# Cross-attention on one core: the order of a slot's work, of its fill and of its end

## The chip, the cores and the metric

The kernel runs on one core of a Trainium2 chip. The metric is the time of one execution on the device in microseconds (us). Several executions are timed and their median is given; one more execution is profiled, and its page and trace are what is read here. The engines are called TensorE (PE, with its weight loads PEld), VectorE (DVE), ScalarE (ACT), GpSimd (POOL) and SyncE (SP), which issues most of the DMAs.

## The reference, cut to what matters

```python
# x: (32, 512, 640) float32, read as hidden_states: 32 batches, 512 rows, 640 columns
# ctx_2048: (32, 77, 1024); all 77 tokens are text, so the other three attentions have no keys
q = _heads(hidden_states @ to_q_w)                      # 20 heads of 32
h_txt = _sdpa(q, _heads(ehs_txt @ to_k_w), _heads(ehs_txt @ to_v_w))   # softmax over 77 keys
out = _merge(h_txt) @ to_out_w + to_out_b
out = out + residual                                    # residual = hidden_states
```

In and out are float32. The kernel gets near that precision by splitting each operand into a high and a low part and adding three products (high x high, high x low, low x high).

## The kernel before

**Tiles and slots.** After a first part that computes the keys and values of all 32 batches and writes them to scratch memory (`k_dram`, `v_dram`; groups of 512 context rows, `LAST` the fifth and shorter one), the kernel walks through 160 slots: `b, j = divmod(n, 5)`, where b is the batch and j one of five chunks of 128 columns, that is four heads. One call of `slot(n)` issues, for chunk n, the scores and exps of four query tiles of 128 rows, and around them work of other chunks, so that the engines overlap:

- `queries(n + 1, ...)`: 15 products into the bank `pq`; `split_q(n + 1)` then makes `qt`: a copy on ScalarE, two partition-crossing copies on GpSimd (L458) and two subtractions on VectorE (L460). `scores(n + 1, 0)` at the head of the next slot needs all of them.
- `scores(n, t)`, t = 0 to 3: three products into a tile `sc` (three buffers), and the row maximum `nm` on VectorE; `exps(n, t)`: four activations on ScalarE that also sum the rows (`sms`).
- `sums(n - 1)`: the reciprocal `rs` on VectorE. `normalize(n - 1, rs)`: one multiplication of `pn` by it on GpSimd (L511). `transpose_p(n - 1)`: VectorE transposes `pn` into `z`, and SyncE stores it in four DMAs to `pd`.
- `load_p(n - 3)`: SyncE loads that chunk back, transposed, into `raw` (two buffers). In the next slot this chunk is `taken` (`takes`: four slots after its scores): `cast_p` (ScalarE, a small and a large cast into `pp`, one buffer), `last_p` (GpSimd, L556: the low part of the small piece), `rest_p` (VectorE, L549: the low part of the large piece), then `values(taken)`.
- `values(m)`: six products into the bank `pa` (one buffer), in the order of `PASSES`: passes 1 and 2 need the casts, 3 and 4 need `last_p`, 5 and 6 need `rest_p`. `sum_a(m)`: a copy `aw` on ScalarE (L581) and two additions on VectorE (L583). In the next slot `high_a(m)` (ScalarE, L590) and `low_a(m)` (VectorE, L595) split the result into `at` and free the bank.
- The output projection: `piece(b, i)` issues products of `at` and `wo_s` into `po` (L613), two pieces per slot; `PIECES` tells which of an earlier batch. The first piece of j=3 ends with the chunk taken in the slot before. `finish()` adds `po` to the residual rows `xr` on VectorE (L642) and stores them.
- `load_residual(b, t)`: SyncE loads 128 rows of x into `xr` (L602, three buffers), one of the four t in each of the slots j=1, 3, 4 and 0 (`RESIDUAL`). `add_bias(b, t)`: GpSimd adds the output bias to them (L606), in the slots that `BIAS` names.
- For the next batch: `refill` issues the key and value loads of half the heads or segments at two places of a slot (`load_keys` eight, `load_values` eight DMAs a group), `copy_keys` copies keys on GpSimd (L423, L424), `load_x`, `transpose_x` and `split_x` prepare its queries' operand.

**What sets the order.** The order is written out by hand: under `tc.manual_schedule` every engine executes its instructions as the program issues them, and SyncE issues its DMAs in that order, each after the one eight before it has landed. The tables show the assignment to slots (a pair is how many batches back, and which t):

```python
RESIDUAL = {1: (1, 0), 3: (1, 1), 4: (1, 2), 0: (2, 3)}
BIAS = {2: (1, 0), 4: (1, 1), 0: (2, 2), 1: (2, 3)}
```

**Fill and end.** The first three slots also compute values of the last context group (`beside`, `context_values`). `LATE` = 3 is the first slot that uses the tiles of the later stage. From slot 8 on there is output work as well (`has_out`). `end()` works off what is left after slot 159: the last four chunks' casts, values and projections.

Of the kernel before, what the change touches and what calls it, by code (L numbers as in the profile page):

```python
# [8 lines left out]
F32 = mybir.dt.float32  # L9
FPR = mybir.dt.float32r  # L10
AF = mybir.ActivationFunctionType
ALU = mybir.AluOpType
# [11 lines left out]
P = 128  # L24
# [27 lines left out]
def kernel(  # L52
# [154 lines left out]
    def split_keys(g, j):  # L207
        g0, gn = GROUPS_KV[g]
        ks = kvt.tile([P, 2, G], FPR, tag="ks", name="ks")
        split(ks[:, 0, :gn], ks[:, 1, :gn], pks.pop(j)[:, :gn])  # L210
        engine = nc.gpsimd if g + 1 < len(GROUPS_KV) else nc.sync
        j0 = GROUPS[GROUP_OF[j]][0]
        engine.dma_start(
            k_dram[GROUP_OF[j]][:, :, j - j0, g0 : g0 + gn].bitcast(F32), ks[:, :, :gn].bitcast(F32)
        )
# [177 lines left out]
    raws, pps, ats, pds, sms, pqs, pas, xrs, pos = ({} for _ in range(9))  # L393
# [115 lines left out]
    def normalize(n, rs):  # L509
        pf = pnb[n % 2][:, :, :NKEY]  # L510
        nc.gpsimd.tensor_tensor(  # L511
            pf, pf, rs.unsqueeze(2).to_broadcast([P, NQ * HPC, NKEY]), ALU.mult
        )
# [24 lines left out]
    def cast_p(n):  # L538

        raw = raws[n]  # L540
        pp = late[0].tile([P, 5, S], FPR, tag="pp", name="pp", bufs=1)
        nc.scalar.copy(pp[:64, 4, :], raw[:64, 2, :])  # L542
        nc.scalar.copy(pp[:, 0:2, :], raw[:, 0:2, :])  # L543
        pps[n] = pp
# [19 lines left out]
    def values(n):  # L564
        b, j = divmod(n, NC_)
        g = GROUP_OF[j]
        pp, vb = pps.pop(n), vbs[g][:, j - GROUPS[g][0]]
        pas[n] = late[1].tile([P, 2, S], F32, tag="pa", name="pa", bufs=1)
        for p, t, c in PASSES:
            nc.tensor.matmul(  # L570
                pas[n][:, p, :],
                vb[:, p, t, :],
                pp[:, c, :],
                start=(c == p),
                stop=(c == p + 2),
            )

    def sum_a(n):
        pa = pas[n]
        aw = late[0].tile([64, 2, S], F32, tag="aw", name="aw", bufs=1)  # L580
        nc.scalar.copy(aw, pa[64:])  # L581
        for p in range(2):
            nc.vector.tensor_tensor(pa[64 * p : 64 * p + 64, 0], pa[:64, p], aw[:, p], ALU.add)  # L583

    def high_a(n):
        if n >= N - NC_ + 1:
            at = xpool[0].tile([P, 2, S], FPR, tag="xt", name="at", bufs=7)
        else:
            at = late[0].tile([P, 2, S], FPR, tag="at", name="at", bufs=8)
        nc.scalar.copy(at[:, 0, :], pas[n][:, 0])  # L590
        ats[n] = at
# [13 lines left out]
    def add_bias(b, t):  # L605
        nc.gpsimd.tensor_tensor(xrs[b, t], xrs[b, t], bias, ALU.add)  # L606
# [21 lines left out]
    def piece(b, i):  # L628
        for t, h, j in STEPS[CUTS[i] : CUTS[i + 1]]:
            if j == 0:  # L630
                output_bank(b, t, h)
            project(b, t, h, j)
            if j == NC_ - 1:
                closed.append((b, t, h))
# [24 lines left out]
    BIAS = {2: (1, 0), 4: (1, 1), 0: (2, 2), 1: (2, 3)}  # L659
    TRANSPOSE_X = {0: ((), (), (0,)), 1: ((1,), (), (2,)), 2: ((3,), (), ())}  # L660
    SPLIT_X = {2: ((0,), (1,)), 3: ((2, 3), (4,))}

    WO = {1: (0, 1, 2), 2: (3, 4)}
    wos = []
# [7 lines left out]
    def refill(b, j, part):  # L672

        heads = range(2 * part, 2 * part + 2)
        segments = SEGMENTS[4 * part : 4 * part + 4]
        if j == 0:
            if not part and b and b + 1 < B:
                load_x(b + 1, (3,))
            load_keys(b, 1, heads)
        elif j == 1 and b:  # L680
            load_values(b - 1, 1, segments)
        elif j == 2:
            load_values(b, 0, segments)
        elif j == 3 and b + 1 < B:
            load_keys(b + 1, 0, heads)

    def slot(n, beside=()):
# [8 lines left out]
        filling = taken is not None and not has_out  # L696
        if not filling:
            refill(b, j, 0)
        copied = {1: 1, 4: 0 if more else None}.get(j)
        if has_out and copied is not None:  # L700
            copy_keys(copied)
        if taken is not None and j != NC_ - 1:
            cast_p(taken)
        if n - 1 in takes:
            high_a(takes[n - 1])
        if taken is not None and j == NC_ - 1:
            cast_p(taken)
        bias_now = j in BIAS and b >= BIAS[j][0]
        if bias_now and not ahead:
            add_bias(b - BIAS[j][0], BIAS[j][1])  # L710
# [3 lines left out]
        rs = sums(n - 1) if n else None  # L714
        if taken is not None:
            last_p(taken)
        if not has_out and copied is not None:
            copy_keys(copied)
        if n:
            normalize(n - 1, rs)  # L720
        exps(n, 0, *s)
        if ahead:
            queries(n + 1, 0, 2)
        if j == NC_ - 1 and n - 1 in takes:
            low_a(takes[n - 1])
        s = scores(n, 1)
        if taken is not None:
            rest_p(taken)
        if j != NC_ - 1 and n - 1 in takes:
            low_a(takes[n - 1])  # L730
        if n == LATE:
            nc.sync.dma_start(bias, bo.unsqueeze(0).to_broadcast([P, C]))
        if n >= LATE:
            load_p(n - LAG + 1)
# [30 lines left out]
        if ahead:  # L765
            split_q(n + 1)
            if bias_now:
                add_bias(b - BIAS[j][0], BIAS[j][1])
            exps(n, 2, *s)
# [18 lines left out]
        if taken is not None and not (early and j == 4):  # L788
            values(taken)
        if len(beside) > 0:  # L790
            context_values(LAST, beside[0], psv)
        if has_out:
            s = scores(n, 3)
            transpose_p(n - 1)
# [3 lines left out]
        if taken is not None:  # L798
            sum_a(taken)
        for c in xsplits[1]:  # L800
            split_x(b + 1, c)
        exps(n, 3, *s)
        if len(beside) > 1:
            context_values(LAST, beside[1], psv)
# [5 lines left out]
    def end():  # L810
# [4 lines left out]
        load_values(last, 1)  # L815
        load_residual(last - 1, 3)
# [3 lines left out]
        high_a(N - 5)  # L820
        last_p(N - 4)
        rest_p(N - 4)
        transpose_p(N - 1)
        low_a(N - 5)
        add_bias(last - 1, 2)
        add_bias(last - 1, 3)
        load_p(N - 2)
# [7 lines left out]
        def turn(n):  # L835
            sum_a(n)
            cast_p(n + 1)
            high_a(n)
            last_p(n + 1)
            rest_p(n + 1)  # L840
            low_a(n)

        turn(N - 4)
        load_p(N - 1)
        load_residual(last, 0)
        load_residual(last, 1)
        piece(last - 1, 8)
        finish()
        values(N - 3)
        piece(last - 1, 9)  # L850
# [22 lines left out]
        for i in range(4):  # L873
            begin(i, 0, 2)
# [4 lines left out]
        for i in range(4):  # L879
            begin(i, 2, 3)  # L880
        for i in (4, 5):
            begin(i, 0, 3)
        take(N - 1)
        for i in range(6):
            begin(i, 3, 4)
# [14 lines left out]
    load_keys(0, 0)  # L900
    load_x(1)
    copy_keys(0)
    for vb in vbs:
        nc.gpsimd.memset(vb.bitcast(F32), 0.0)
    queries(0, 0, NC_)
    split_q(0)
# [8 lines left out]
    psv.release()  # L915
    kvp.release()
    late.append(ctx.enter_context(tc.tile_pool(name="late", bufs=1, reuse_waits="tile")))
    late.append(
        ctx.enter_context(tc.tile_pool(name="psl", bufs=1, space=PSUM, reuse_waits="tile"))
    )  # L920
# [43 lines left out]
```

## Time and profile before

| | before |
|---|---|
| times of three runs, us | 1944.38, 1933.45, 1927.69 (median 1933.45) |
| profiled execution: its time, its span, us | 1923.57, 1921.7 |
| mean granted TensorE clock | 0.992 |
| busy, us: PE, DVE, ACT, POOL | 1883.1, 1626.7, 1526.3, 1422.3 |
| weight loads (PEld) busy, us | 1665.2 |
| HBM read and written | 247.17 MB, 181.64 MB (223 GB/s) |

Busy times are unions of the spans of an engine's instructions; TensorE's products are pipelined and their ends modelled, so that its 98% hides small waits, which are read better from the distance between the starts of its instructions. `x` before a number counts instructions; in a timeline row the first two numbers are start and length in us, and the bracket at its end tells how long the engine stood idle before it and what ended that.

### The profile page before, as it was taken

How to read it: one execution, taken by the hardware profiler on the slowest of the kernel's cores; microseconds unless marked ns; L12 is line 12 of the kernel's file. 1: busy time of each engine (PE TensorE's matmuls, PEld its weight loads, DVE VectorE, ACT ScalarE, POOL GpSimd, SP SyncE). 2: the span in 40 equal slices, each digit the busy share in tenths (PEclk: the TensorE clock that was granted, in tenths of full speed). 3: DMA queues.
4: the chain of work that ended last, by engine and by line, in shares of the span. 5: the costliest groups of instructions: out<-in, count | busy, mean ns of one | idle time of the engine just before them, and what ended most of it. 6: DMA issues, size and time to landing. Idle time of an engine off the chain costs nothing.

```text
span 1921.7 us, 37548 instructions
## 1 busy us (share of the span) xinstructions
PE 1883.1 (98%) x10332; PEld 1665.2 (87%) x10332; DVE 1626.7 (85%) x2494; ACT 1526.3 (79%) x6210; POOL 1422.3 (74%) x1116
## 2 busy tenths in 40 slices
PE   9999997999999999999999999999999999999998
PEld 7888886888888888888888889888888888888887
DVE  5444447899999989999999999999999999999985
ACT  3232247998998989899888899998998989999882
POOL 1100067888898888888888888888888888888873
PEclk9999998999999999999999999999999999999999
DMA  9878869898888888888989898898889888889875
GB/s 185 201 195 249 200 176 222 215 233 238 235 232 233 233 216 231 233 231 228 238 223 236 236 239 234 232 237 231 234 228 233 225 240 234 237 232 229 226 211 157
DMA packets 565022, 431.36 MB, mean 224 GB/s; under 512 B 191120, under 2 KB 473168, under 8 KB 564816
## 3 DMA queue, kind: packets, MB, share of 16 engines
q1 hardware_dynamic: 560304, 414.47, 84.0%
q0 software_dynamic: 4416, 14.34, 2.2%
q8 instruction: 85, 1.39, 0.3%
q14 instruction: 121, 0.99, 0.2%
q10 hardware_dynamic: 96, 0.16, 0.0%
HBM read 247.17 MB, written 181.64 MB: 223 GB/s over the span
## 4 chain that ended last, share of the span: by engine, by line
PE 44%; ACT 15%; DVE 14%; DMA 13%; issue 5%; SPq 5%; POOL 3%; DVEq 0%; POOLq 0%; ACTq 0%
PE pq L443 11%; PE po L613 11%; PE pv L191 6%; DMA raw<-pd 6%; ACT pn L496 6%; PE pk L191 6%; PE pa L570 5%; PE sc L478 4%; DVE pp L549 4%; DMA xs<-in_x_dram 3%; ACT pp L543 2%; DVE nm L486 2%; DVE z L518 2%; ACT xt L264 2%; ACT aw L581 2%
## 5 line engine op out<-in xcount | busy, mean ns | idle before, releaser
L496 ACT ACTIVATE pn<-sc,nm 128x77 f32<-128x77 f32 x2560 | 794.0, 333 | 32.6 <-DVE nm L486 27.7
L613 PE MATMUL po<-wo_s,at 128*128 128x320 f32 x3840 | 636.1, 314 | 7.3 <-DVE at L595 3.0
L443 PE MATMUL pq<-xt,wq_s 128*128 128x512 f32 x2400 | 621.4, 400 | 0.0
L613 PEld LDWEIGHTS po<-wo_s,at 128*128 128x128 f32 x3840 | 569.0, 189 | 15.9 <-DVE at L595 12.3
L496 ACT ACTIVATION_READ_ACCUMULATOR pn<-sc,nm 128x1 f32 x2560 | 545.7, 213 | 0.0
L511 POOL TENSOR_TENSOR pn<-pn,rs 128x1232 f32<-128x1232 f32 x160 | 503.5, 3147 | 23.8 <-DVE rs L506 12.3
L443 PEld LDWEIGHTS pq<-xt,wq_s 128*128 128x128 f32 x2400 | 429.9, 190 | 75.7
L478 PEld LDWEIGHTS sc<-kb,qt 128*128 128x128 f32 x1920 | 327.9, 189 | 59.7 <-POOL qt L458 12.1
L478 PE MATMUL sc<-kb,qt 128*128 128x154 f32 (+1 forms) x1920 | 317.9, 274 | 13.8 <-POOL qt L458 8.9
L486 DVE TENSOR_REDUCE nm<-sc 128x4 f32<-128x308 f32 x640 | 288.4, 451 | 44.1 <-PE sc L478 37.6
L549 DVE TENSOR_TENSOR pp<-raw,pp 128x1024 fp32r<-128x1024 f32 x160 | 261.1, 1632 | 31.0 <-ACT pp L543 24.9
L556 POOL TENSOR_TENSOR pp<-raw,pp 64x512 fp32r<-64x512 f32 x160 | 212.4, 1327 | 97.5 <-ACT pp L542 88.5
L570 PE MATMUL pa<-pp,vb 128*128 128x512 f32 x960 | 265.5, 407 | 10.0 <-DVE at L595 6.2
L518 DVE STREAM_TRANSPOSE z<-pn 128x1280 f32<-128x1280 f32 x160 | 241.9, 1512 | 8.0 <-DMA pd<-z 2.8
L583 DVE TENSOR_TENSOR pa<-pa,aw 64x512 f32<-64x512 f32 x320 | 222.7, 696 | 21.1 <-ACT aw L581 10.8
L460 DVE TENSOR_TENSOR qt<-pq,qt 64x512 fp32r<-64x512 f32 x320 | 219.2, 685 | 23.6 <-ACT qt L454 17.0
L265 POOL TENSOR_TENSOR xt<-xs,xt 128x512 fp32r<-128x512 f32 x160 | 202.6, 1292 | 34.0 <-ACT xt L264 30.7
L570 PEld LDWEIGHTS pa<-pp,vb 128*128 128x128 f32 x960 | 171.8, 190 | 57.8 <-DVE pp L549 13.2
L606 POOL TENSOR_TENSOR xr<-xr,bias 128x640 f32<-128x640 f32 x128 | 202.7, 1584 | 17.6 <-DMA xr<-in_x_dram 6.0
L458 POOL CAST qt<-qt 64x512 fp32r<-64x512 f32 x320 | 195.0, 609 | 21.7 <-ACT qt L454 2.0
L581 ACT COPY aw<-pa 64x1024 f32<-64x1024 f32 x160 | 161.9, 1012 | 47.5 <-PE pa L570 43.3
L542 ACT CAST pp<-raw 64x512 fp32r<-64x512 f32 x160 | 99.5, 622 | 97.6 <-DMA raw<-pd 97.3
(46 smaller groups left out, 1639.8 us busy)
## 6 DMA issues: line engine op xcount, KB each, us to landing
pd<-z SPq DMA_DIRECT2D x640, 160.0 KB, 3.5
raw<-pd SPq DMA_DIRECT2D x160, 512.0 KB, 4.0
xs<-in_x_dram SPq DMA_DIRECT2D x128, 320.0 KB, 7.2
xr<-in_x_dram SPq DMA_DIRECT2D x128, 320.0 KB, 3.8
out_dram<-xr SPq DMA_DIRECT2D x127, 320.0 KB, 3.7
raw<-pd SPq DMA_DIRECT2D x160, 128.0 KB, 4.2
v_dram<-vs SPq DMA_DIRECT2D x80, 192.0 KB, 4.1
k_dram<-ks POOLq DMA_DIRECT2D x20, 512.0 KB, 4.3
```

The costliest lines, as they stand in the source:

```text
L191: nc.tensor.matmul(held[j][:, :gn], w[:, k, a, :], cts[g, k][:, c, :gn], start=(k == 0 and n == 0), stop=(k == NK - 1 and n == 2),)
L443: nc.tensor.matmul(pqs[n], wq_s[:, k, a, j * P : (j + 1) * P], xts[b, k][:, c, :], start=(k == 0 and m == 0), stop=(k == NC_ - 1 and m == 2),)
L460: nc.vector.tensor_tensor(qt[r, 1 + w, :], pq[r], qt[r, 0, :].bitcast(F32), ALU.subtract)
L478: nc.tensor.matmul(sc[:, cols], qt[:, m, t * P : (t + 1) * P], keys_, start=(m == 0), stop=(m == 2),)
L486: nc.vector.tensor_reduce(nm, sc[:, :KCOLS].rearrange("p (h k) -> p h k", k=NKEY), AX.X, ALU.max, negate=True)
L496: nc.scalar.activation(pnb[n % 2][:, at, :NKEY], sc[:, i * NKEY : (i + 1) * NKEY], AF.Exp, bias=nm[:, i : i + 1], accum_out=sms[n][:, at : ...
L511: nc.gpsimd.tensor_tensor(pf, pf, rs.unsqueeze(2).to_broadcast([P, NQ * HPC, NKEY]), ALU.mult)
L518: nc.vector.transpose(z.rearrange("p b t j -> p t b j"), pn.rearrange("p (t h) k -> p t (h k)", t=NQ).rearrange("p t (b i) -> p t b i", i=Q),)
L549: nc.vector.tensor_tensor(pp[:, 2:4, :], raw[:, 0:2, :], pp[:, 0:2, :].bitcast(F32), ALU.subtract)
L570: nc.tensor.matmul(pas[n][:, p, :], vb[:, p, t, :], pp[:, c, :], start=(c == p), stop=(c == p + 2),)
L583: nc.vector.tensor_tensor(pa[64 * p : 64 * p + 64, 0], pa[:64, p], aw[:, p], ALU.add)
L613: nc.tensor.matmul(pos[b, t, h][:, :HALF], ats[b * NC_ + j][:, a, t * P : (t + 1) * P], wos[0][:, j, c, h * HALF : (h + 1) * HALF], start= ...
```

## The change

It moves work in time and between queues; the products, their number and the bytes moved stay the same.

- Steady slots: `low_a` is issued ahead of `rest_p` on VectorE, and in j=3 `high_a` between the two casts on ScalarE. The fourth score tile stands between passes 4 and 5 of the value products (not in j=4). `sum_a` is parted into `copy_a` and `add_a`; after j=4, 0 and 1 the reciprocal `sums(n)` is taken in the same slot, ahead of `add_a`. `normalize` is two multiplications of half the heads each; it goes ahead of `last_p` in j=1 and j=2, and in j=4 its second half goes behind the query copies. In j=1 `copy_keys` goes behind `last_p`.
- `BIAS`: (b-2, 3) moves from j=1 to j=0, and (b-1, 0) from j=2 to j=1. `RESIDUAL` stays. `SPLIT_X`: in j=2 both splits stand at the first place.
- Fill: key loads of both groups at the start; the query copies ahead of `copy_keys`; `split_values` of the last group one slot after its products; two `wo` loads move from slot 2 to slots 5 and 6; the first probability loads go earlier; the last group's key stores of j=3 and 4 are issued by ScalarE.
- End: the stores of the last `z` and a probability load go ahead of eight value loads, `low_a` goes forward, and the projection pieces are cut differently.

```diff
@@ split_keys
-        engine = nc.gpsimd if g + 1 < len(GROUPS_KV) else nc.sync
+        engine = nc.gpsimd if g + 1 < len(GROUPS_KV) else nc.sync if j < 3 else nc.scalar
@@
-    def normalize(n, rs):
-        pf = pnb[n % 2][:, :, :NKEY]
-        nc.gpsimd.tensor_tensor(
-            pf, pf, rs.unsqueeze(2).to_broadcast([P, NQ * HPC, NKEY]), ALU.mult
-        )
+    def normalize(n, rs, halves=(0, 1)):
+        half = NQ * HPC // 2
+        for k in (i * half for i in halves):
+            pf = pnb[n % 2][:, k : k + half, :NKEY]
+            nc.gpsimd.tensor_tensor(
+                pf, pf, rs[:, k : k + half].unsqueeze(2).to_broadcast([P, half, NKEY]), ALU.mult
+            )
@@ cast_p
         nc.scalar.copy(pp[:64, 4, :], raw[:64, 2, :])
+        if between is not None:
+            between()
         nc.scalar.copy(pp[:, 0:2, :], raw[:, 0:2, :])
@@
-    BIAS = {2: (1, 0), 4: (1, 1), 0: (2, 2), 1: (2, 3)}
+    BIAS = {4: ((1, 1),), 0: ((2, 2), (2, 3)), 1: ((1, 0),)}
-    SPLIT_X = {2: ((0,), (1,)), 3: ((2, 3), (4,))}
-    WO = {1: (0, 1, 2), 2: (3, 4)}
+    SPLIT_X = {2: ((0, 1), ()), 3: ((2, 3), (4,))}
+    WO = {1: (0, 1, 2), 5: (3,), 6: (4,)}
@@ slot
+        if n > LATE and not has_out:
+            load_p(n - LAG + 1)
...
-        if has_out and copied is not None:
+        if has_out and copied == 0:
             copy_keys(copied)
+            copied = None
...
+        if taken is not None and j < 4:
+            cast_p(taken, high if has_out and j == 3 else None)
+        if not (has_out and j == 3):
+            high()
...
-        rs = sums(n - 1) if n else None
+        if n and n - 1 not in rss:
+            rss[n - 1] = sums(n - 1)
+        if has_out and j in (1, 2):
+            normalize(n - 1, rss.pop(n - 1))
         if taken is not None:
             last_p(taken)
-        if not has_out and copied is not None:
+        if copied is not None:
             copy_keys(copied)
-        if n:
-            normalize(n - 1, rs)
+        parted = j == 4 and has_out and ahead
+        if n - 1 in rss:
+            normalize(n - 1, rss[n - 1], (0,) if parted else (0, 1))
...
         s = scores(n, 1)
+        if j != NC_ - 1 and n - 1 in takes:
+            low_a(takes[n - 1])
         if taken is not None:
             rest_p(taken)
-        if j != NC_ - 1 and n - 1 in takes:
-            low_a(takes[n - 1])
...
             split_q(n + 1)
-            if bias_now:
-                add_bias(b - BIAS[j][0], BIAS[j][1])
+            if parted:
+                normalize(n - 1, rss.pop(n - 1), (1,))
+            for bias_of in biases:
+                add_bias(*bias_of)
             exps(n, 2, *s)
...
-            values(taken)
+            values(taken, 0, 4 if has_out else 6)
...
             s = scores(n, 3)
+            if j != 4:
+                values(taken, 4, 6)
             transpose_p(n - 1)
...
-        if taken is not None:
-            sum_a(taken)
+        if has_out:
+            copy_a(taken)
...
-        exps(n, 3, *s)
...
+        if has_out:
+            exps(n, 3, *s)
+        if has_out and j in (4, 0, 1):
+            rss[n] = sums(n)
+        if taken is not None:
+            add_a(taken)
@@ end
-        load_values(last, 1)
-        load_residual(last - 1, 3)
...
+        load_p(N - 2)
+        load_residual(last - 1, 3)
         transpose_p(N - 1)
-        low_a(N - 5)
+        load_values(last, 1)
@@ start of the slots
     load_keys(0, 0)
+    load_keys(0, 1)
     load_x(1)
+    queries(0, 0, NC_)
+    split_q(0)
     copy_keys(0)
     for vb in vbs:
         nc.gpsimd.memset(vb.bitcast(F32), 0.0)
-    queries(0, 0, NC_)
-    split_q(0)
```

## The prediction

> **What bounds the kernel now.** I read the page first, then the busy time by stage, then TensorE's timeline slot by slot. A slot is one (batch, chunk of 128 columns), numbered n, with j = n mod 5. From the page:
>
> ```profile
> PE 1883.1 (98%) x10332; PEld 1665.2 (87%) x10332; DVE 1626.7 (85%) x2494; ACT 1526.3 (79%) x6210; POOL 1422.3 (74%) x1116
> ```
>
> From the busy time by stage (length, then PE, PEld, DVE, ACT, POOL, the granted clock, DMA share, GB/s):
>
> ```profile
> 303.00:307.00 4.00, 3.82 (x11) 3.04 (x11) 1.66 (x3) 0.95 (x7) 3.92 (x4) 0.50 0.86 219
> ...
> 316.00:320.00 4.00, 3.14 (x12) 2.60 (x13) 3.52 (x6) 3.98 (x17) 2.89 (x4) 0.83 1.08 209
> 320.00:323.00 3.00, 3.00 (x11) 2.38 (x10) 3.00 (x3) 1.89 (x13) 1.75 (x1) 0.66 0.97 195
> ...
> 800.00:1000.00 200.00, 199.08 (x1132) 176.94 (x1132) 187.93 (x287) 179.83 (x758) 171.73 (x131) 1.00 0.88 232
> ```
>
> From slot 10 on TensorE is the bound; whatever makes it wait lengthens the run by as much. How much it waits, TensorE's timeline tells: taking a slot from its first score product to the next slot's, slots 10 to 158 last on average 9.84 us for j=0, 10.03 for j=1, 10.05 for j=2, 10.22 for j=3 and 10.15 for j=4. They hold the same products, so j=0 is the full-speed slot, and the others wait 0.19, 0.21, 0.38 and 0.30 us: 1.08 us per batch, 32 us in 30 batches. That is all the steady state has to give. Three rows of the timeline show where:
>
> ```profile
> 836.60 1.64 PE L570 MATMUL pa<-pp,vb 128*128 128x512 f32 x6
> ...
> 838.40 1.96 PE L613 MATMUL po<-wo_s,at 128*128 128x320 f32 x12
> ...
> 854.80 2.33 PE L613 MATMUL po<-wo_s,at 128*128 128x320 f32 x12
> ...
> 865.93 1.84 PE L570 MATMUL pa<-pp,vb 128*128 128x512 f32 x6
> ```
>
> In j=3 twelve output products take 2.33 instead of 1.96 us, since the last three need `low_a`'s result; in j=4 the value products take 1.84 instead of about 1.6, since passes 5 and 6 need `rest_p`'s.
>
> **Part 1, the low part first, and the score tile amid the value products.** On VectorE `low_a` (0.68 us) stood behind `rest_p` (1.2 to 2.3 us) in j=0 to 3; it now comes first, and in j=3 `high_a` goes between the two casts. In slot 57 (j=2) `low_a` ended at 6.37 us of the slot and the value products, which write the bank that it reads, began at 6.43; in slot 58 (j=3) it ended at 6.38, while the output products that end with its result had begun at 4.53. Now it ends 1.2 to 2.1 us earlier. `rest_p` ends 0.7 us later, at about 6.4 to 6.8, but only passes 5 and 6 read it, and these now start behind four passes (0.94) and a score tile (0.33), at 6.31 + 1.27 = 7.6. So the waits of j=2 and j=3 go: 0.59 x 30 = -18 us. In j=4 all six passes still come in one piece and the casts are not moved; its 0.30 I leave. Bounds: 0 and -27 (j=4's as well). ScalarE's copy of `pa` can start 0.33 us later; in j=1 to 3 it begins 0.8 to 1.3 us after the products anyway.
>
> **Part 2, the sooner bias.** Before, `add_bias` of (b-2, 3) was GpSimd's last work of slot j=1. It now stands in j=0, behind the bias of (b-2, 2) and ahead of everything GpSimd does for j=1. But its rows `xr` are loaded in that same slot j=0 (RESIDUAL is not changed), and SyncE issues that load late. SyncE in slot 55 (j=0, from 820.47; slot 56 begins at 830.29):
>
> ```profile
> 821.43 2.92 SPq L525 DMA_DIRECT2D pd<-z  x4
> 824.39 0.99 SPq L253 DMA_DIRECT2D xs<-in_x_dram  x1
> 825.48 2.27 SPq L419 DMA_DIRECT2D kb<-k_dram  x4
> 827.86 0.38 SPq L534 DMA_DIRECT2D raw<-pd  x1
> 828.29 0.48 SPq L535 DMA_DIRECT2D raw<-pd  x1
> 828.86 1.94 SPq L419 DMA_DIRECT2D kb<-k_dram  x4
> 830.85 0.43 SPq L602 DMA_DIRECT2D xr<-in_x_dram  x1
> ```
>
> Fifteen transfers stand ahead of it, back to back from the moment `z` is transposed, and the change moves none of them. The query for `xr` in that stretch gives 4.1 us to landing: 834.96, which is 4.67 us into slot 56. GpSimd in the same stretch:
>
> ```profile
> 828.40 1.57 POOL L606 TENSOR_TENSOR xr<-xr,bias 128x640 f32<-128x640 f32 x1
> 829.92 0.44 POOL L423 CAST kb<-kb 64x308 fp32r<-64x308 f32 x1
> 833.02 0.44 POOL L424 CAST kb<-kb 64x308 fp32r<-64x308 f32 x1 [2.67 <-DMA kb<-k_dram]
> 833.54 1.29 POOL L556 TENSOR_TENSOR pp<-raw,pp 64x512 fp32r<-64x512 f32 x1
> 834.91 3.14 POOL L511 TENSOR_TENSOR pn<-pn,rs 128x1232 f32<-128x1232 f32 x1
> ```
>
> GpSimd already waits here, for the key transfer just ahead of `xr`, and TensorE does not feel it. In the changed order GpSimd does bias (b-2, 2) until 829.97, waits for `xr` until 834.96, and then does bias 1.57, normalise 3.14 (now ahead of `last_p` in j=1 and 2) and `last_p` 1.29: it ends at 834.96 + 6.00 = 840.96. Queued behind this wait are `last_p`, for which passes 3 and 4 of the value products wait, then `copy_keys` (needed two slots later) and the query copies of slot 57. Pass 3 ran at 837.14 here (two passes after 836.60), so TensorE stands 3.8 us. The same sum for all 30 batches, each with its own landing and durations, gives 3.28 us on average (1.6 to 4.5; the load lands 2.4 to 5.8 us into slot j=1, and only one landing before 0.8 us would be in time). GpSimd catches up: the query copies end at 840.96 + 0.9 + 1.3 = 843.2, while the delayed slot ends at 844.0. So +3.28 x 30 = +98 us. Bounds: 1.6 and 4.5 in every batch, +48 and +136.
>
> **Part 3, the clock after the stall.** No row of the steady state shows a stall this long; the nearest are in the fill:
>
> ```profile
> 302.98 0.49 PE L478 MATMUL sc<-kb,qt 128*128 128x154 f32 x1 [2.59 <-POOL qt L458]
> ...
> 303.94 2.85 PE L443 MATMUL pq<-xt,wq_s 128*128 128x512 f32 x6
> ```
>
> Six products take 2.85 instead of 1.6 us, at a clock of 0.50. The wait of 2.2 us at 316.5 is followed by 0.83 in 4 us and 0.66 in 3, that is 1.36 + 2.04 = 3.4 us at half speed, 1.7 us lost. Of the four waits around 2 us or more (before 264.7, 303.0, 312.2, 316.5) two were followed by it. The new one is longer than all of them: I take 0.7 x 1.7 = 1.2 us, +36 us in 30 batches; bounds 0 and 1.7, +51.
>
> [...]
>
> **Part 4, the fill.** Slots 0 to 9 wait 26 us beyond full speed. The query copies go ahead of the key copies and memsets, which removes the 2.23 and 0.33 us before slot 0's second and third score products (the wait on `POOL qt`): about 2.6. The first probability load gets ahead of three DMAs (the bias, and two `wo` loads moved to slots 5 and 6, needed in slot 8) and ScalarE's 5.4 us wait for it at 309.3 shrinks; but GpSimd's v_dram issues (2.6 us) still stand ahead of slot 4's query copies. I take -10; bounds 0 and -26.
>
> **Part 5, the end.** The last stores of `z` go ahead of eight value loads (about 0.47 us each on SyncE, 3.8), and output products cover the last `turn`s, where TensorE waits 1.4, 1.2, 1.2 and 1.3 us. Against that, the value loads land as much later. I take -3; bounds +3 and -9.
>
> **At nothing:** normalise in two halves (one more GpSimd instruction per slot; GpSimd is 86% busy between 800 and 1000); in j=4 the second half behind the query copies, which holds the `z` transpose from 9.54 to about 10.0; `sums` ahead of `add_a` on VectorE, which then waits for the last exps. Together these make slot j=0's query copies end about 0.6 us later, 8.4 instead of 7.85, with 9.83 needed: 1.4 us of cover. If it is gone, each 0.1 us costs 3 us.
>
> **Sum.** Against the profiled execution's 1923.57 us: -18 + 98 + 36 - 10 - 3 = +103, 2026.6. The median of the runs shown, 1933.45, is 9.9 above that execution: 2036.5, rounded to 2036.
>
> **Rivals.** (a) *The stall without the clock* (15%): 2036 - 36 = 2000. For it: two of four waits went without; against: this one is longer. (b) *GpSimd does not catch up* (6%) and the next slot's query copies or `last_p` come late too: its margin in slot 57 is 0.8 us; at a further 2 us per batch, 2036 + 60 = 2096. Against: j=2 now has no bias. (c) *The bias load is in time* (9%), the case on the other side: part 2 and 3 fall away, and the rest gives 1933.45 - 31 = 1902. Place: GpSimd ahead of j=1's normalise; it decides if `xr` lands before 0.78 us of slot j=1 (6.78 less 1.57, 3.14 and 1.29), which needs SyncE some 3.5 us ahead of where it was. Against: 30 of 30 loads landed later, and the fifteen transfers at 0.43 us or more each take over 6 us after `z`.
>
> **How the numbers follow.** The forecast with stall and clock has 70%. A measurement of this kernel can tell about 1% from no change. Slower by over 1% are the forecast and rivals (a) and (b), 91%, less a little for a stall far smaller than the rows say: 0.90; faster by over 1% is most of (c): 0.07; the rest, 0.03, is within 1%. Around 2036, the bounds of part 2's mean (about 0.7 us per batch, 21 us), of the clock (25), of part 1 (13), of the fill and end (11) add to 37 as independent errors; I reach to 1985 for (a) with a good fill, and to 2080.
>
> **What would show it.** Right: among GpSimd's waits, L617 on the DMA of `xr` with about 30 entries of some 4 to 5 us; TensorE waiting at the value products on GpSimd's `last_p` (L560) once per batch; slots j=1 of 13 us or more, often followed by half clock; j=2 and j=3 near 9.85. Wrong: no such wait, the `xr` load early on SyncE, or a stall that is taken up in front of pass 3.

## The result and the profile after

The changed kernel takes 2058.15 us (median of 4 runs, 2057.50 to 2058.88) against 1938.37 us before (4 runs, 1927.69 to 1944.38): a ratio of 1.0617, 95% interval 1.0592 to 1.0642. Its profiled execution took 2057.87 us, with a span of 2056.0 and a mean clock of 0.967. From the page, the busy times and one group of instructions (busy, mean ns of one, idle before them and what ended it):

```profile
PE 1917.6 (93%) x10332; PEld 1703.7 (83%) x10332; DVE 1665.3 (81%) x2494; ACT 1538.2 (75%) x6210; POOL 1390.0 (68%) x1276
...
L575 PE MATMUL pa<-pp,vb 128*128 128x512 f32 x960 | 302.7, 425 | 115.7 <-POOL pp L560 111.0
```

TensorE's share fell from 98% to 93%, though it is busy 34 us longer (at half clock products took about twice as long: in slot 56 passes 5 and 6 start 0.51 us apart at half clock, passes 1 and 2 0.24 at full). Of its 138 us of idle time 115.7 have one address: the value products `pa`, nearly always waiting for GpSimd's `last_p` (L560). Behind that stands the bias. The waits of the whole run (total, times, longest):

```profile
POOL xr L617 <- DMA xr<-in_x_dram: 152.8, 45, 6.4
...
PE pa L575 <- POOL pp L560: 111.0, 34, 4.7
```

One occurrence, in slot 56 (j=1, from 873.11; its predecessor from 863.26). SyncE issues the load of `xr` last of the row, behind the key loads, as before:

```profile
871.74 1.95 SPq L419 DMA_DIRECT2D kb<-k_dram  x4
873.74 0.42 SPq L613 DMA_DIRECT2D xr<-in_x_dram  x1
```

GpSimd adds the bias of (b-2, 2), then stands 4.33 us for that load, and only then does the bias of (b-2, 3), the normalise and `last_p`:

```profile
871.56 1.57 POOL L617 TENSOR_TENSOR xr<-xr,bias 128x640 f32<-128x640 f32 x1
877.46 1.56 POOL L617 TENSOR_TENSOR xr<-xr,bias 128x640 f32<-128x640 f32 x1 [4.33 <-DMA xr<-in_x_dram]
878.99 3.38 POOL L513 TENSOR_TENSOR pn<-pn,rs 128x616 f32<-128x616 f32 x2
882.45 1.26 POOL L560 TENSOR_TENSOR pp<-raw,pp 64x512 fp32r<-64x512 f32 x1
```

TensorE does passes 1 and 2 and stands 3.69 us ahead of pass 3, until `last_p` ends at 883.71:

```profile
879.44 0.63 PE L575 MATMUL pa<-pp,vb 128*128 128x512 f32 x2
883.76 1.05 PE L575 MATMUL pa<-pp,vb 128*128 128x512 f32 x2 [3.69 <-POOL pp L560]
...
886.14 2.48 PE L624 MATMUL po<-wo_s,at 128*128 128x320 f32 x12
```

After it comes 3.4 us at half clock. Busy time by stage (length, PE, PEld, DVE, ACT, POOL, granted clock, DMA share, GB/s):

```profile
882.30:884.00 1.70, 0.24 (x1) 0.24 (x2) 0.64 (x1) 0.36 (x3) 1.56 (x3) 0.99 0.98 351
884.00:887.40 3.40, 3.40 (x12) 3.01 (x12) 1.93 (x2) 0.96 (x1) 2.62 (x5) 0.50 0.51 129
887.40:888.50 1.10, 1.10 (x10) 1.10 (x9) 0.06 (x1) 1.07 (x8) 0.81 (x1) 1.00 0.13 29
```

The slot lengths, measured as in the prediction (first score product to first score product, slots 10 to 158, mean us), for every kernel of this study. The order is that of the sections below; the last column is TensorE's time at half clock between slots 10 and 159.

| kernel | j=0 | j=1 | j=2 | j=3 | j=4 | half clock, us |
|---|---|---|---|---|---|---|
| before | 9.84 | 10.03 | 10.05 | 10.22 | 10.15 | 0 |
| after | 9.84 | 15.30 | 9.93 | 9.85 | 9.96 | 109.2 |
| bias_back | 9.83 | 9.90 | 9.96 | 10.36 | 11.42 | 0 |
| only_t0_sooner | 9.85 | 9.85 | 14.78 | 9.89 | 9.90 | 92.2 |
| only_t3_sooner | 9.84 | 15.03 | 9.89 | 9.85 | 10.12 | 105.8 |
| load_first | 9.83 | 10.16 | 10.17 | 10.55 | 11.43 | 0 |
| array_busy | 9.82 | 13.81 | 9.85 | 9.85 | 10.74 | 0 |
| bias_back_whole | 9.83 | 9.85 | 9.88 | 9.90 | 11.07 | 0 |
| bias_back_splits | 9.82 | 9.90 | 9.91 | 10.02 | 11.39 | 0 |
| bias_back_sums | 9.84 | 10.09 | 10.76 | 9.87 | 10.36 | 0 |
| part1_alone | 9.85 | 10.30 | 11.07 | 10.60 | 11.45 | 0 |
| bias_alone | 9.94 | 12.76 | 10.13 | 9.87 | 9.93 | 44.4 |
| whole_splits | 9.83 | 9.88 | 9.89 | 9.89 | 11.12 | 0 |
| part1_fill_end | 9.83 | 9.92 | 10.04 | 9.85 | 11.09 | 0 |

The two spans differ by 134.3 us. Slots 10 to 158 give 137.7 of them (1498.6 to 1636.3), the stretch before slot 10 gives 3.1, and the end gives 6.5 back (57.5 to 51.0).

### The profile page after: what moved, and what is told of

The parts are those of the page before. It is cut to its first block, busy times and chain, and to the rows that moved or that the text cites. A ratio compares the mean times of both kernels' runs of the same rounds, so it can differ in the third digit from the quotient of the medians.

```text
span 2056.0 us, 37657 instructions
## 1 busy us (share of the span) xinstructions
PE 1917.6 (93%) x10332; PEld 1703.7 (83%) x10332; DVE 1665.3 (81%) x2494; ACT 1538.2 (75%) x6210; POOL 1390.0 (68%) x1276
## 3 DMA queue, kind: packets, MB, share of 16 engines
q10 hardware_dynamic: 640, 1.02, 0.1%
## 4 chain that ended last, share of the span: by engine, by line
PE 35%; DVE 15%; ACT 14%; DMA 13%; POOL 12%; issue 7%; SPq 5%; POOLq 0%; DVEq 0%; ACTq 0%
PE po L624 9%; PE pq L443 8%; POOL pn L513 7%; ACT pn L496 6%; PE pk L191 5%; PE pv L191 5%; PE pa L575 4%; DMA raw<-pd 4%; DVE pp L553 3%; PE sc L478 3%; POOL pp L560 3%; DVE z L520 3%; DMA pd<-z 3%; DMA xs<-in_x_dram 3%; DVE pa L590 2%
## 5 line engine op out<-in xcount | busy, mean ns | idle before, releaser
L624 PE MATMUL po<-wo_s,at 128*128 128x320 f32 x3840 | 648.3, 320 | 0.7 <-ACT at L601 0.6
L624 PEld LDWEIGHTS po<-wo_s,at 128*128 128x128 f32 x3840 | 604.8, 197 | 14.7 <-ACT at L601 0.7
L513 POOL TENSOR_TENSOR pn<-pn,rs 128x616 f32<-128x616 f32 x320 | 477.9, 1511 | 34.7 <-DVE rs L506 18.5
L575 PE MATMUL pa<-pp,vb 128*128 128x512 f32 x960 | 302.7, 425 | 115.7 <-POOL pp L560 111.0
L478 PEld LDWEIGHTS sc<-kb,qt 128*128 128x128 f32 x1920 | 333.7, 193 | 63.1 <-POOL qt L458 12.4
L478 PE MATMUL sc<-kb,qt 128*128 128x154 f32 (+1 forms) x1920 | 323.7, 277 | 14.8 <-POOL qt L458 8.6
L617 POOL TENSOR_TENSOR xr<-xr,bias 128x640 f32<-128x640 f32 x128 | 204.4, 1598 | 178.4 <-DMA xr<-in_x_dram 152.8
L553 DVE TENSOR_TENSOR pp<-raw,pp 128x1024 fp32r<-128x1024 f32 x160 | 290.5, 1816 | 17.3 <-ACT pp L547 13.0
L265 POOL TENSOR_TENSOR xt<-xs,xt 128x512 fp32r<-128x512 f32 x160 | 202.7, 1292 | 78.1 <-issue 33.4
L560 POOL TENSOR_TENSOR pp<-raw,pp 64x512 fp32r<-64x512 f32 x160 | 207.6, 1297 | 54.6 <-ACT pp L544 33.7
L547 ACT CAST pp<-raw 128x1024 fp32r<-128x1024 f32 x160 | 168.6, 1054 | 0.0
```

Source lines behind the costliest of these rows:

```text
L478: nc.tensor.matmul(sc[:, cols], qt[:, m, t * P : (t + 1) * P], keys_, start=(m == 0), stop=(m == 2),)
L513: nc.gpsimd.tensor_tensor(pf, pf, rs[:, k : k + half].unsqueeze(2).to_broadcast([P, half, NKEY]), ALU.mult)
L553: nc.vector.tensor_tensor(pp[:, 2:4, :], raw[:, 0:2, :], pp[:, 0:2, :].bitcast(F32), ALU.subtract)
L560: nc.gpsimd.tensor_tensor(pp[64:, 4, :], raw[:64, 2, :], pp[:64, 4, :].bitcast(F32), ALU.subtract)
L575: nc.tensor.matmul(pas[n][:, p, :], vb[:, p, t, :], pp[:, c, :], start=(c == p), stop=(c == p + 2),)
L624: nc.tensor.matmul(pos[b, t, h][:, :HALF], ats[b * NC_ + j][:, a, t * P : (t + 1) * P], wos[0][:, j, c, h * HALF : (h + 1) * HALF], start= ...
```

## The experiments

Ratios are against runs of the kernel before on the same chip, with 95% intervals. The kernel before itself takes 1937 us (median) on the chip of the first four experiments and 1920 to 1921 on the chips of the others, so times of different experiments are compared by these ratios.

**Is it the bias?** `bias_back`: the changed kernel with the old table.

```diff
-    BIAS = {4: ((1, 1),), 0: ((2, 2), (2, 3)), 1: ((1, 0),)}
+    BIAS = {2: ((1, 0),), 4: ((1, 1),), 0: ((2, 2),), 1: ((2, 3),)}
```

> The changed kernel with the old bias table (each bias one slot later, where it stood before), all else as changed. Theory A (GpSimd waits for the DMA of the residual rows, ahead of the work that the value products need): the stall of 3.74 us and the half clock behind it (1.7 us) go in all 30 batches, and the stall of slot 7 in the fill as well; 2058 - 163 - 6 = about 1889 us, slots j=1 at 9.9 us. Rival B (normalise ahead of last_p in j=1 and 2, and sums ahead of add_a, make last_p late; the bias is only in the way): last_p still stands behind normalise, so most of the loss stays, over 2000 us.

Measured: 1951.98 us, 1.0068 (1.0046 to 1.0091). The stall and all half clock between slots 10 and 159 are gone, so the table is the cause of both. But the time is not 1889: j=4 rises from 9.96 to 11.42. A second loss had been hidden by the first.

**Which of the two moved biases?** `only_t0_sooner` moves (b-1, 0) from j=2 to j=1 alone, `only_t3_sooner` (b-2, 3) from j=1 to j=0 alone.

```diff
+    BIAS = {4: ((1, 1),), 0: ((2, 2),), 1: ((2, 3), (1, 0))}     # only_t0_sooner
+    BIAS = {2: ((1, 0),), 4: ((1, 1),), 0: ((2, 2), (2, 3))}     # only_t3_sooner
```

> Of the two biases that the change moves, only (b-1, 0) is sooner (j=1 instead of j=2, behind that of (b-2, 3), which is back in j=1). Theory A: its rows are loaded in j=1 and landed 3.45 us into j=2 before, so GpSimd waits there in the same way: 3.45 + 1.57 + 3.3 + 1.3 = 9.6 against 6.8, a stall of 2.8 us, plus 1.7 of half clock, in 31 batches: 1889 + 140 = about 2030 us, the long slots now j=2, near 14.3 us. Rival C (only the bias of (b-2, 3) hurts, since only its load comes late): 1889 us.

> Only (b-2, 3) is sooner (j=0 instead of j=1); (b-1, 0) is back in j=2. Theory A: slots j=1 as in the changed kernel, 15.3 us with a stall of 3.7; slot 7 of the fill without its stall: 2058 - 6 = about 2052 us. Rival D (the two biases only together overfill GpSimd): well under 2000 us.

Measured: 2035.39, 1.0499 (1.0468 to 1.0529), with the stall in j=2; and 2055.77, 1.0601 (1.0575 to 1.0628), with the stall in j=1. By the medians one alone costs 98 us and the other 119, against 120 for both. In the changed kernel the second has little left to wait for: in slot 56 the load of (b-1, 0) is issued at 883.60 and GpSimd stands 0.60 us ahead of that bias at 886.64, after the stall.

**Is it the load or the place?** `load_first` keeps (b-2, 3) in j=0 and issues its load at the head of that slot; (b-1, 0) is back in j=2, as in `only_t3_sooner`.

```diff
+        if j == 0 and b >= 2:
+            load_residual(b - 2, 3)
...
-        if j in RESIDUAL and b >= RESIDUAL[j][0]:
+        if j in RESIDUAL and j != 0 and b >= RESIDUAL[j][0]:
```

> As the kernel with only (b-2, 3) sooner, but SyncE issues the load of those rows at the head of slot j=0, ahead of the x and key loads (eleven transfers earlier). Theory A: it lands near 8.5 us of slot j=0, before GpSimd's turn at 9.9: no stall, about 1889 us, although the bias stands where the change put it. Rival B' (the 1.57 us of bias work ahead of normalise and last_p are themselves the loss): at least 1.57 x 30 = 47 us stay, 1936 us or more.

Measured: 1975.42, 1.0192 (1.0166 to 1.0218). The load now lands 0.18 us before the start of j=1 on average, and GpSimd does both biases in a row without a wait (slot 56 begins at 843.56):

```profile
842.01 3.11 POOL L617 TENSOR_TENSOR xr<-xr,bias 128x640 f32<-128x640 f32 x2
```

With the load in time the stall is gone (j=1 10.16, no half clock): the wait was for the load. But the time is not 1889: again j=4 is at 11.43, and here j=3 at 10.55. It is also 23 us above `bias_back`, which differs only in the place of this bias and of its load: the place costs something without the stall too, though not the 1.57 us per batch of rival B' in j=1 (0.26 more than in `bias_back`).

**What is the clock's share?** `array_busy`: the changed kernel with 14 additional products in j=1 ahead of the value products, into the bank that pass 1 then overwrites, so that TensorE idles less in the stall.

```diff
+        if busy:
+            for _ in range(14):
+                nc.tensor.matmul(
+                    pas[n][:, 0, :], vb[:, 0, 0, :], pp[:, 0, :], start=True, stop=True
+                )
```

> The changed kernel with 14 extra products ahead of the value products of every slot j=1 from slot 11 on (3.3 us; they write the bank that pass 1 then overwrites, so the result is the same), so that TensorE works through most of the stall. Theory A (half the clock for 3.4 us after each stall costs 1.7 us): the half clock of 109 us between slots 10 and 159 goes, and with it some 50 us: 2058 - 50 = about 2008 us, slots j=1 at 13.6 us. Rival H (the half clock costs nothing, since other engines are as late): 2058 us or more.

Measured: 2030.50, 1.0572 (1.0547 to 1.0597). Half clock between slots 10 and 159 goes from 109.2 us to 0 and j=1 from 15.30 to 13.81: 1.49 us per batch, near the expected figure. `last_p` ends at the same place of slot j=1 in both (10.54 and 10.55 us), and from there to the next slot it is 4.76 us at half clock and 3.26 without: the difference is the clock's alone. But the time is not the 2008 expected, since j=4 takes 0.78 of it back: `rest_p` ends about 1.0 us later of the slot in j=2, 3 and 4 than in the changed kernel. So the long slot j=1 was also time in which other engines caught up. The net gain is 24 us by the slots of the two profiles and some 9 by the ratios (1.0617 and 1.0572); the changed kernel was not run beside this one, so its size stays open.

**What is the second loss?** Three versions of `bias_back`, each with one more edit undone: the normalise of j=4 in one piece, both splits of x at their old places, the sums behind `add_a`.

```diff
-        parted = j == 4 and has_out and ahead
+        parted = False                                            # bias_back_whole
-    SPLIT_X = {2: ((0, 1), ()), 3: ((2, 3), (4,))}
+    SPLIT_X = {2: ((0,), (1,)), 3: ((2, 3), (4,))}                # bias_back_splits
-        if has_out and j in (4, 0, 1):
-            rss[n] = sums(n)
         if taken is not None:
             add_a(taken)
+        if has_out and j in (4, 0, 1):                            # bias_back_sums
+            rss[n] = sums(n)
```

> As bias_back (1952 us, slots j=3 and 4 at 10.4 and 11.4), but with normalize of j=4 whole and ahead of the query copies, where it stood before. Theory E (the parted normalize makes the transpose to z 0.5 us late, SyncE with it, the probability loads land late in j=2, ScalarE falls behind until j=4): j=3 and j=4 go back to near 9.9, about 1900 us. Rivals F and G (the two x splits at one place in j=2; the reciprocal ahead of add_a): it stays at 1945 us or more.

> As bias_back, but with the second x split of j=2 behind the copy of pa on ScalarE, where it stood before. Rival F (two splits ahead of that copy hold the copy and the last exps of j=2 by 0.6 us, and j=3 and 4 behind them): j=4 from 11.4 to near 10.2, 1952 - 36 - 12 = about 1905 us. Theories E and G: 1945 us or more.

> As bias_back, but VectorE takes the reciprocal sums(n) of j=4, 0 and 1 behind add_a instead of ahead of it. Theory G (add_a waits for the last exps through the reciprocal, high_a and ScalarE's queue behind it 0.4 us later in every slot): add_a 0.4 us earlier, j=3 and 4 shorter, about 1915 us. Theories E and F: 1945 us or more.

Measured: 1924.83, 1.0027 (1.0011 to 1.0043); 1937.80, 1.0081 (1.0064 to 1.0099); 1936.00, 1.0066 (1.0041 to 1.0091). By the ratios the parted normalise is part of the loss, the splits are not, and the sums move it from j=4 (10.36) to j=2 (10.76). Over 11 us in j=4 remain in the first two, so the main cause is another. `whole_splits` (the first two together) and `part1_fill_end` (that, with the sums and the normalise in their old places too) looked for a better version:

```diff
-    SPLIT_X = {2: ((0, 1), ()), 3: ((2, 3), (4,))}
+    SPLIT_X = {2: ((0,), (1,)), 3: ((2, 3), (4,))}                # whole_splits, on bias_back_whole
-        if has_out and j in (1, 2):
-            normalize(n - 1, rss.pop(n - 1))
-        if has_out and j in (4, 0, 1):
-            rss[n] = sums(n)                                      # part1_fill_end, on whole_splits
```

> The changed kernel with three edits undone: the bias back in j=1 and j=2, the normalise of j=4 in one piece, and the splits of x in j=2 at two places again; nothing left out. Theory P (the parted normalise and the two splits together make the loss that the bias hid): j=4 falls from 11.07 to about 10.1 us, j=0 to 3 stay at 9.85 to 9.95, some 30 us less than with the splits, about 1.5% below before, ratio 0.985. Theory Q (the splits are not it): j=4 stays above 10.9 and the ratio above 0.998.

> The changed kernel without its small edits in the steady slots: besides the three edits of whole_splits, the sums and the normalise stand where they were before. What is left is part 1, the fill and the end; nothing left out. Theory P (the parts add up where nothing stands in GpSimd's way): part 1 alone's gain of about 18 us, some 4 us in the fill and 5 to 6 at the end, about 1.5% below before, ratio 0.985. Theory Q (the earlier sums are needed to get part 1's gain): j=1 to j=3 stay between 10.0 and 10.3 us and the ratio is 0.995 or more, above that of whole_splits.

Measured: 1924.73, 1.0018 (1.0003 to 1.0033); 1927.69, 1.0029 (1.0014 to 1.0044). In both j=4 stays at 11.1, and neither beats the kernel before.

**Part 1 by itself.** `part1_alone` is the kernel before with `low_a` ahead of `rest_p`, `high_a` between the casts in j=3 and the score tile amid the value products; the normalise stays one instruction.

```diff
-            cast_p(taken)
-        if n - 1 in takes:
-            high_a(takes[n - 1])
+            cast_p(taken, high if has_out and j == 3 else None)
+        if not (has_out and j == 3):
+            high()
...
+        if j != NC_ - 1 and n - 1 in takes:
+            low_a(takes[n - 1])
         if taken is not None:
             rest_p(taken)
-        if j != NC_ - 1 and n - 1 in takes:
-            low_a(takes[n - 1])
...
-            values(taken)
+            values(taken, 0, 4 if has_out else 6)
...
             s = scores(n, 3)
+            if j != 4:
+                values(taken, 4, 6)
```

> The kernel before with part 1 alone (the low part ahead of rest_p, the high part between the casts in j=3, the fourth score tile amid the value products); nothing left out. Theory P (part 1 is worth what its waits cost): slots j=2 and j=3 fall from 10.05 and 10.22 to about 9.85 us, the others stay, about 18 us less than before, ratio 0.991. Theory Q (part 1's gain isn't there without the slack that the stall gives): the slots shorten by under 0.1 us on average and the ratio is 0.997 to 1.003.

Measured: 2014.57, 1.0494 (1.0474 to 1.0513). Both theories are wrong: a part that I had priced at -18 us costs 94 by itself (its three edits were not run one at a time). Here the second loss stands alone and can be read. Groups of instructions between 370 and 1860 us, `rest_p` and the normalise, of the kernel before:

```profile
L549 DVE TENSOR_TENSOR pp<-raw,pp 128x1024 fp32r<-128x1024 f32 x148 | 242.3, 1637 | 25.4 <-ACT pp L543 22.4 <-DMA pd<-z 2.3
...
L511 POOL TENSOR_TENSOR pn<-pn,rs 128x1232 f32<-128x1232 f32 x149 | 475.6, 3192 | 20.6 <-DVE rs L506 11.9
```

and of `part1_alone`:

```profile
L551 DVE TENSOR_TENSOR pp<-raw,pp 128x1024 fp32r<-128x1024 f32 x140 | 345.4, 2467 | 14.6 <-ACT pp L545 10.8
...
L511 POOL TENSOR_TENSOR pn<-pn,rs 128x1232 f32<-128x1232 f32 x140 | 362.7, 2591 | 39.6 <-DVE rs L506 32.4
```

The same two instructions: VectorE's is 0.83 us longer, GpSimd's 0.60 shorter. In the timeline one sees why. Slot 57 (j=2) before, VectorE and then GpSimd:

```profile
844.77 1.20 DVE L549 TENSOR_TENSOR pp<-raw,pp 128x1024 fp32r<-128x1024 f32 x1
```

```profile
844.65 3.45 POOL L511 TENSOR_TENSOR pn<-pn,rs 128x1232 f32<-128x1232 f32 x1 [0.72 <-DVE rs L506]
```

and in `part1_alone`, where `low_a` (L598) comes between:

```profile
869.45 0.67 DVE L598 TENSOR_TENSOR at<-pa,at 128x512 fp32r<-128x512 f32 x1
870.04 2.65 DVE L551 TENSOR_TENSOR pp<-raw,pp 128x1024 fp32r<-128x1024 f32 x1
```

```profile
869.34 2.28 POOL L511 TENSOR_TENSOR pn<-pn,rs 128x1232 f32<-128x1232 f32 x1 [0.18 <-DVE rs L506]
```

In these rows the two instructions exclude each other. Before, `rest_p` started 0.12 us after the normalise, ran its 1.20 us, and the normalise took 2.28 + 1.17. Now it starts 0.70 us after it, waits until the normalise ends at 871.62, and ends 1.07 later. So it is nearly everywhere from 360 us on: of the `rest_p`s before that started within a normalise (42, on average 0.11 us after it), all took 1.20 us; in `part1_alone` 100 of 112 waited it out (started 0.53 us after it on average), took 2.83, and the normalise took its bare 2.28. `low_a` runs its 0.67 us within the normalise undisturbed (0.67 to 0.68 us in all 115 cases of the kernel before that lie within one, 0.68 in the two that met no instruction of GpSimd); one of its two inputs is in PSUM, but that this is the reason was not shown.

Slot j=2 pays at once: the prediction had passes 5 and 6 start at 7.6 us of the slot, `rest_p` now ends at 8.66 on average, and the slot is 1.02 us longer. From there it goes on down VectorE's queue: the row maximum of the third tile behind `rest_p`, then that tile's exps. Waits between 370 and 1860 us before, and 370 and 1900 in `part1_alone`:

```profile
ACT pn L496 <- DVE nm L486: 21.6, 75, 0.7
```

```profile
ACT pn L496 <- DVE nm L486: 174.1, 132, 2.1
```

In j=3 the ScalarE copies of x stand behind those exps, and GpSimd's splits need these copies: the first copy ends 1.12 us before the start of j=4 in the kernel before, 0.04 before it in `whole_splits` and 0.30 after it in `part1_alone`, and the first split starts at -0.86, 0.09 and 0.44 us of j=4. The slot j=4 pays most (1.31 us in `part1_alone`): there GpSimd does the three splits (L265), two key copies and `last_p` in a row, and `rest_p` waits for `last_p` in the same way. Slot 59 before (from 860.49), GpSimd and VectorE:

```profile
859.60 3.79 POOL L265 TENSOR_TENSOR xt<-xs,xt 128x512 fp32r<-128x512 f32 x3
...
864.61 1.29 POOL L556 TENSOR_TENSOR pp<-raw,pp 64x512 fp32r<-64x512 f32 x1
```

```profile
864.71 2.28 DVE L549 TENSOR_TENSOR pp<-raw,pp 128x1024 fp32r<-128x1024 f32 x1 [0.38 <-ACT pp L543]
```

and of `whole_splits` (slot 59 from 857.57):

```profile
857.48 3.80 POOL L265 TENSOR_TENSOR xt<-xs,xt 128x512 fp32r<-128x512 f32 x3 [0.37 <-POOL qt L458]
...
862.50 1.30 POOL L560 TENSOR_TENSOR pp<-raw,pp 64x512 fp32r<-64x512 f32 x1
```

```profile
862.75 2.14 DVE L553 TENSOR_TENSOR pp<-raw,pp 128x1024 fp32r<-128x1024 f32 x1 [0.38 <-ACT pp L547]
```

The splits begin 0.89 us before the slot's start in the one, 0.09 before it in the other; `rest_p` ends at 6.50 against 7.32 of the slot, and passes 5 and 6, and the slot, end as much later (10.13 and 10.95). In each of the 14 profiles `rest_p` ends on average 1.08 us after `last_p` in j=4, and the slot's length follows its end: 6.01 and 9.94 us in the changed kernel, 6.51 and 10.15 before, 7.48 and 11.11 in `whole_splits`, 7.82 and 11.45 in `part1_alone` (without the first six batches). That GpSimd's order in j=3 and j=4 is the bound is read from these rows; a version that moves a split was not run.

What makes part 1 bearable without the stall is, by these rows, the normalise in two halves of 1.23 us, which lets `rest_p` in between them. In `part1_fill_end`, which has it, the same group is

```profile
L553 DVE TENSOR_TENSOR pp<-raw,pp 128x1024 fp32r<-128x1024 f32 x147 | 241.8, 1645 | 16.0 <-ACT pp L547 15.8 <-DMA pd<-z 0.3
```

and where it waits for a half it takes 1.65 us (60 cases), against 2.83 for a whole one in `part1_alone`. The slots sum to 50.73 us per batch instead of 53.27. (That kernel also has `copy_keys` behind `last_p` in j=1, and the new fill and end; the halves alone were not added to `part1_alone`.)

**The bias by itself.** `bias_alone` is the kernel before with the new table; `last_p` stands ahead of the normalise.

> The kernel before with the new table BIAS alone: (b-2, 3) from j=1 to j=0 and (b-1, 0) from j=2 to j=1; nothing left out. Theory P (GpSimd waits for the load of xr whatever stands around it): j=1 between 14.5 and 15.5 us with half clock of over 80 us in all, the time 125 to 145 us above before, ratio 1.065 to 1.075. In this order last_p stands ahead of the normalise and so the stall should be some 3 us shorter where the load lands alike: Theory Q therefore puts the loss at 10 to 60 us, ratio 1.005 to 1.03, with j=1 at 10.5 to 12 us, and says that the normalise ahead of last_p is half of the damage.

Measured: 1986.96, 1.0352 (1.0322 to 1.0383), between the two theories. Its waits:

```profile
POOL xr L606 <- DMA xr<-in_x_dram: 169.6, 44, 7.3
...
PEld pa L570 <- POOL pp L556: 71.9, 32, 3.8
```

The load lands as late as in the changed kernel (4.20 us into j=1 against 4.16), but behind the bias stand only the key copies and `last_p`. From the landing to the end of `last_p` it takes 4.70 us instead of 6.38, and the stall is 2.02 us on average instead of 3.74. So some 1.7 us of the stall come with the normalise ahead of `last_p`, and the rest with the late load (the two kernels differ in part 1 too). With the stall and without part 1, j=3 (9.87) and j=4 (9.93) are as short here as in the changed kernel. Half clock follows in 13 of 30 batches: 44 us instead of 109.

## Why the prediction was right, and where not

The forecast, 2036 with the stall and the clock, named the mechanism, and the time lies in its range. Its signs in the profile came too: L617 waits for the load of `xr` (45 times), j=1 is at 15.30, j=2 and j=3 at 9.93 and 9.85. Its sum was +103 us; the spans differ by 134.3. The medians differ by 119.8 only, since before's profiled execution lay below all of its timed runs; that this made up for part of the error is luck.

- **Part 2, the stall: 98 forecast, 112.2 measured** (3.74 us on average in 30 batches, 1.97 to 4.89, against 3.28, 1.6 to 4.5; from the start of pass 2 to that of pass 3, less the 0.235 us of an undisturbed pass). The load landed 4.16 us into j=1, near the 4.26 of before. What was too small was the work behind it: from the landing to the end of `last_p` it was 6.38 us instead of the 6.00 counted, and in slot 56 the normalise in halves took 3.38 of that instead of 3.14.
- **Part 3, the clock: 36 forecast, 51 measured** (3.43 us at half clock per batch after the stall, half of it lost). The factor of 0.7 was wrong: of the 30 stalls of the changed kernel 28 were followed by half clock, so the term stands at its upper bound. Seven of these 28 stalls left TensorE idle for less than the 3.41 us of one half-clock stretch, one for 2.73 us (more on this in the last section). `array_busy` confirms the size within slot j=1 with 1.49 us.
- **Part 1: -18 forecast; slots shorter by 26 us, of which little is part 1's.** In the changed kernel j=2, 3 and 4 are shorter by 0.12, 0.37 and 0.19, and the 0.18 that j=1 waited before is gone. But in `bias_alone`, with the stall and without part 1, j=3 and j=4 are as short; only j=2 (10.13 there, 9.93 here) is left for part 1 and the other edits, some 6 us. That the term looks right beside the stall is luck: alone, part 1 costs 94 us. The step that failed is "`rest_p` ends 0.7 us later, at about 6.4 to 6.8". In `part1_alone` it ends at 6.53, 7.43, 8.66 and 7.90 of j=0 to 3, where before it ended at 4.36, 5.46, 5.65 and 5.76. I had added the length of `low_a` and not asked which instruction of GpSimd would hold `rest_p` up at its new start. "In j=4 ... its 0.30 I leave" failed too: j=4 is where most of it is paid.
- **At nothing:** the normalise in halves was counted as one more instruction. By the comparison of `part1_alone` with `part1_fill_end` it is most of what keeps part 1 from costing 94 us. Its parting in j=4 costs some of j=3 and j=4 when no stall covers it (10.02 and 11.39 in `bias_back_splits` against 9.89 and 11.12 in `whole_splits`; 1.0081 against 1.0018). The cover in j=0 held: j=0 stays between 9.82 and 9.94 in every kernel.
- **Part 4: -10 forecast, +3.1 measured.** Slot 0 gained 3.05 us, near the 2.6 for the query copies, and slot 4 gained 3.3; but the sooner bias strikes in the fill too. In slot 7 GpSimd stands 5.9 us ahead of L617, whose load was issued 3.3 us before it, TensorE stands 1.8 us ahead of `pa`, and slots 7 and 8 are 6.7 us longer. Without the sooner bias the stretch from the first score to slot 10 (103.4 us before) is 103.9 in `bias_back`, 102.9 in `part1_fill_end` and 101.2 in `whole_splits`; where the rest of the 10 went was not tried.
- **Part 5: -3 forecast, -6.5 measured**; `part1_fill_end` (51.9) and `whole_splits` (50.8) have it too, `part1_alone` (57.4) does not.
- **The rivals.** (a) fell with the clock. (b) fell: j=2 is at 9.93. (c), the load in time, was run as `load_first`: 1.0192, about 1970 on the prediction's scale and not 1902. Its place and condition were right; its price took the rest of the change for a gain of 31 us, where by itself it costs 15 (`bias_back`).

So the parts don't add up. By the medians, each against the kernel before beside it, the new table alone costs 67 us and the rest of the change alone 15 (`bias_back`), which is 82; together they cost 120. And the 26 us of the other slots stand only beside a slot j=1 that is 5.3 us longer, in which the other engines catch up: filled with products, and 1.5 us shorter, it gave 0.78 back in j=4.

## What to carry to other kernels

A step moved ahead of another on VectorE can change which engine's instruction goes first: in `part1_alone` `low_a` ahead of `rest_p` put it behind the normalise, 2.83 us instead of 1.20. Before pricing such a move, look up what GpSimd runs at the new start, and take that instruction's end plus about the own length for the price of losing (here 1.08 us behind the end, of 1.20). A sum of parts that is made beside a large stall says nothing of what the parts are worth without it: next to the stall j=3 and j=4 got shorter with part 1 and without it, and part 1 alone cost 94 us. And before a consumer is moved forward in a queue, its load has to be moved first, ahead of the transfers that it stands behind.

## What the runs showed of the hardware

**Half clock began on a grid of 3.413 us, after windows of it that were idle for about half their length or more.** Where the trace shows half clock, it begins on a grid of 3.413 us. I added up TensorE's idle time in each window of that grid, in the profiles of before, after, `only_t3_sooner`, `only_t0_sooner`, `bias_alone` and `bias_back` from 300 us on: of 2714 full-speed windows with under 1.5 us idle none was followed by a window at half clock; of 87 with 1.9 us or more all were; of 44 between, 16. (The ends of products are modelled, so the idle times are rough.) In these profiles the limit thus lay between 1.5 and 1.9 us, near half a window. It fits the 13 of 30 in `bias_alone`: by these counts its stall of 2.02 us on average is followed by half clock only if most of it falls into one window.

**In the changed kernel half clock came nearly once per batch, mostly 16 windows after the last.** Half-clock stretches begin at 389.05, 443.66, 498.28, 552.89 and 607.50 us: 54.61 apart, 16 windows of 3.413 (two later steps have 17). The batch lasts 54.88 us on average, 16.08 windows, so one stretch per batch on that grid gives such steps by itself. Its four runs lie within 0.07% of each other, those of before within 0.9%; the reason was not shown.

**`rest_p` on VectorE and the normalise or `last_p` on GpSimd excluded each other one by one** (`low_a`, with one input in PSUM, was not held up: 0.67 us within the normalise), with prices that can be read to a hundredth: 1.08 us from the end of `last_p` to the end of `rest_p` in j=4, in 14 kernels. With starts some 0.1 us apart, either won: in slot 57 before, `rest_p` started 0.12 us after the normalise and ran its 1.20 us, and the normalise took 3.45; in slot 59 it started 0.10 us after `last_p`, which took its 1.29, and needed 2.28.
